# A graph attention and expert kernel: own orders for the second, third and last step, and an end split into graphs and half rows

## The chip, the cores and the metric

The kernel runs on one core of a Trainium2 chip. The metric is device time in microseconds (us) from the start to the end of one execution, lower is better. The core has five engines that run side by side, each with a queue of its own in program order: TensorE (PE, matrix products; its weight loads are shown as PEld), VectorE (DVE), ScalarE (ACT), GpSimd (POOL) and SyncE (SP, which issues most transfers).

## The reference, cut to what matters

There are 128 graphs of 128 nodes with 1024 features. Each goes through a graph attention layer and then through a layer of low-rank experts:

```python
x = x + gnn(layernorm(x), adj, W, a)     # 16 heads of 64: softmax over neighbours, att @ Wh, elu
xn = layernorm(x)
gates = softmax of the 2 largest of (xn[:, 0, :] @ router_w.T), of 8 experts
x = x + xn + sum over chosen experts of gate * up(down(xn))      # rank 16
```

The attention score of a neighbour does not depend on the neighbour's own features here, only on the row, so a row's weights reduce to two numbers per head (an exponential for entries and one for absent entries) and the neighbour sum is a product of the 0/1 adjacency with Wh. The routing of a graph takes only its first row.

## The kernel before, in words

**Steps.** A step q (0 to 63) takes two graphs, 2q and 2q+1, through the product with W (1024 x 1024, float32). It is done by seven block products M1 to M7 instead of eight (sums of blocks of x are made by GpSimd, L462; sums of blocks of W lie in SBUF). From step 2 on, two steps share the products M3 and M5, which are split once more by the same scheme: the joint products I and J (L609), whose weight sums `w_in` are made once by GpSimd (`inner_blocks`, L122 to L125, for the blocks T1 and B22). A block product is 16 matmuls at L530 (a and b halves of 8).

**Behind the product.** ScalarE makes the high part of each of four blocks (`hi0` to `hi3`, L683), VectorE the remainder (`lo0` to `lo3`, L687). One step later come, for the two graphs: weights (`aw`, `pe`, `aw2`: L705 to L733), attention product (`A0`, `A1`: L742), scaling by the weights (`h`, L748, in place in PSUM), elu and residual (`x` L755, `e` L758 on ScalarE, `y` L765, `n` on GpSimd), the variance (`q`, L774 on ScalarE), a copy and a DMA transpose (`t`, L815 and L817) and the copy into `y_t` (`rj`, L821), and the second normalization with the residual (`jn`, L842).

**Experts.** Four graphs make a group g. Its routing runs on VectorE (`choose`, L937 to L944), the rows of the chosen experts are fetched by GpSimd's indirect DMA, then follow the down product (`D`, L1004), the gates (`dn`, L1015), the up product (`U0`, `U1` for the two halves of the columns, L1024) and the addition (`v00` to `v11`, L1033) with the store. The last group uses dense weights instead: `load_all` and `load_router` bring all rows in, `order_all` (L1055) reorders the down rows, `down_dense` (L1064), `gates_dense` and `up_dense` (L1089, L1090) do the rest.

**Order.** All five engines are scheduled by hand: the order in which tasks are issued in the program is the order in each engine's queue. Steps 2 to 63 follow two lists, `EVEN` and `ODD`, in which a name ending in `-` belongs to the step before. Steps 0, 1 and 64 to 65 are ordered by `at_the_ends`, which fills eight gaps between the block products. There `weights`, `update` (scaling to mean of one graph) and the rest run graph by graph whole rows at a time, the tables of the experts are centred in one function (`experts`), and both `inner_blocks` stand in step 1.

**PSUM.** Two pairs of banks (`pw0`, `pw1`) belong to the block products; two more pairs (`ps_d`) serve everything else in turn: the attention product of one graph takes a pair, an up product of four graphs both.

```python
if HALVES["left"] is None:
    two = double(name)
    HALVES["left"] = two[:, 1]
    return two[:, 0]
left, HALVES["left"] = HALVES["left"], None
return left
```

Of the kernel before, what the change touches and what calls it, by code (L numbers as in the profile page):

```python
# [18 lines left out]
NO_ENTRY = -3.0e38  # L19
# [3 lines left out]

EVEN = """
# [11 lines left out]
fe5- M2a h0 rj1- jn1- M2b h1 M6a x0 x1 e0 fe2- y0 ps2- fe8- sc0 n0 M6b hi0 e1  # L36
""".split()
# [3 lines left out]
def adj_ffn_kernel(  # L41
# [117 lines left out]
    def load_counts(g):  # L159
        adj_i = work.tile([P, G, N], I32, tag="adj_i", name="adj_i", bufs=1)  # L160
        nc.sync.dma_start(adj_i, adj[g])
        GRP[g] = {"adj_i": adj_i}

    def load_adj(g):
        adj_f = work.tile([P, G, N], F32R, tag="adj_f", name="adj_f")
        nc.gpsimd.dma_start(adj_f, adj_t[g])
        GRP[g]["adj_f"] = adj_f
# [199 lines left out]
    def experts(part, sums):  # L367

        nonlocal down_row, up_row
# [3 lines left out]
        nc.tensor.matmul(pr[:, ER:ER + E], mean_of, sums, start=True, stop=True)  # L373
        nc.vector.scalar_tensor_tensor(
# [5 lines left out]
        nc.sync.dma_start(router_table, router_k.rearrange("p e k -> p (e k)"))  # L380
        down = down_sb.rearrange("p e r k -> p (e r) k")
# [3 lines left out]
                          down_sb.rearrange("p e r k -> p e (r k)"))  # L385
        rows = work.tile([P, P], I32, tag="hp", name="rows")
# [258 lines left out]
    def project(q):  # L645
# [9 lines left out]
        if q:  # L655
            for names in (("M1", "p1"), ("M6", "u2"), ("M2", "hi0", "sc0"), ("M5", "u4"),
                          ("M7", "c22"), ("M3", "c12"), ("M4", "c21")):
                do(names[0] + "a", names[0] + "b", *names[1:])
                yield
            return  # L660
# [30 lines left out]
    def attention_weights(q):  # L691


        g, first = divmod(2 * q, G)
        st = GRP[g]
        shape = [P, 2, H]
        pair = slice(first, first + 2)
        neg = st["neg"][:, pair, None].to_broadcast(shape)
        rstd = RSTD[q]
        e = small.tile(shape, F32, tag="e", name="e", bufs=2)  # L700
        blocks = e.rearrange("p t (h j c) -> p (t h) j c", h=NH, j=2)
        sc = SC.pop(q)
        for dst, raw in (((blocks[:, 1:], WH[q][:, :, :, SCORES]), (blocks[:, 0], sc)) if q
                         else ((e, sc),)):
            nc.vector.scalar_tensor_tensor(dst, raw, ALPHA, raw, op0=ALU.mult, op1=ALU.max)  # L705
# [3 lines left out]
        p = small.tile([P, 2, 2, H], F32, tag="p", name="p", bufs=2)  # L709
        nc.vector.tensor_tensor(p[:, 0], e, m, ALU.subtract)  # L710
        nc.vector.tensor_tensor(p[:, 1], neg, m, ALU.subtract)
        ATT[q] = p

    def exp_weights(q):

        nc.scalar.activation(ATT[q], ATT[q], AF.Exp)

    def divide_weights(q):

        g, first = divmod(2 * q, G)  # L720
        st = GRP[g]
        shape = [P, 2, H]
        pair = slice(first, first + 2)
        p = ATT[q]
        z = small.tile([P, 2, 2, H], F32, tag="z", name="z", bufs=2)
        nc.vector.tensor_mul(z, p, st["n"][:, :, pair, None].to_broadcast(z.shape))
        den = small.tile(shape, F32, tag="den", name="den", bufs=2)


        nc.vector.scalar_tensor_tensor(den, z[:, 0], TINY, z[:, 1], op0=ALU.add, op1=ALU.add)  # L730
        nc.vector.reciprocal(den, den)
        ATT[q] = small.tile(shape, F32, tag="att", name="att")
        nc.vector.tensor_mul(ATT[q], p[:, 0], den)  # L733
# [11 lines left out]
    def weigh_sum(i):  # L745

        ph = PH[i].rearrange("p j (h f) -> p (j h) f", f=F)
        nc.vector.tensor_tensor(ph, ph, ATT[i // 2][:, i % 2, :, None].to_broadcast([P, H, F]),  # L748
# [75 lines left out]
    def turn_at_end(i):  # L824

        two = double("pt")
        TT[i] = [two[:, h].rearrange("p (c n) -> p c n", c=CPH) for h in range(NH)]
        for h, pt in enumerate(TT[i]):
            for c in range(CPH):
                k = h * CPH + c  # L830
                nc.tensor.transpose(pt[:, c, :], X[i][:, k * P:(k + 1) * P], ident)

    def keep_turned(i):
        y = y_of(i)
        for h, pt in enumerate(TT.pop(i)):
            (nc.vector.tensor_copy if h and i == B - 1 else nc.scalar.copy)(
                y[:, h * CPH:(h + 1) * CPH], pt)

# [42 lines left out]
    def turned_parts(g, last):  # L881

        st = GRP[g]
        n = 1 if last else G - 1
        if not last:
            st["add"] = small.tile([P, G * E + G], F32, tag="add", name="add", bufs=1)
        add = st["add"][:, 0:G * E].rearrange("p (g e) -> p g e", g=G)[:, G - 1:G] if last else (
            st["add"][:, 0:(G - 1) * E].rearrange("p (g e) -> p g e", e=E))
        shape = [P, n, E, KC]
        prod = work.tile(shape, F32, tag="hp", name="prod")  # L890
        router = router_all.rearrange("p (o e k) -> p o e k", o=1, e=E)
        if last:
            pieces = [(pt.rearrange("p (o c) n -> p o n c", o=1)[:, :, 0:1],
                       slice(h * CPH, (h + 1) * CPH)) for h, pt in enumerate(TT[g * G + G - 1])]
        else:
            pieces = [(st["y_t"].rearrange("p k (g n) -> p g n k", g=G)[:, 0:n, 0:1],
                       slice(0, KC))]
        for rows, k in pieces:
            part = prod[:, :, :, k]
            nc.vector.tensor_tensor(part, rows.to_broadcast(part.shape),  # L900
                                    router[:, :, :, k].to_broadcast(part.shape), ALU.mult)
        nc.vector.tensor_reduce(add, prod, AX.X, ALU.add)

    def logits(g):
# [4 lines left out]
        if g < NG - 1:  # L909
            nc.tensor.matmul(st["pl"][:, 0:G * E + G], ones, st["add"], start=True, stop=True)  # L910
            return
        nc.tensor.matmul(st["pl"][:, 0:G * E], ones, st["add"][:, 0:G * E], start=True, stop=True)
        down_dense(g, 2, 2, range(0, 5))
        st["dev"] = single("dev")[:, 0:G]
        nc.tensor.matmul(st["dev"], ones, st["add"][:, G * E:], start=True, stop=True)
        down_dense(g, 2, 2, range(5, KC))
# [44 lines left out]
    def weigh(g):  # L961
# [5 lines left out]
        if g < NG - 1:  # L967
            st["gate"] = own(gate, "gate")
# [88 lines left out]
    def down_dense(g, t, n, chunks=range(8)):  # L1057

        st = GRP[g]
        if "pd" not in st:  # L1060
            st["pd"] = slot_of(0)[:, 0]
        cols = slice(t * P, (t + n) * P)
        for k in chunks:
            nc.tensor.matmul(st["pd"][:, cols], down_all[:, k].rearrange("p e r -> p (e r)"),  # L1064
                             st["y_t"][:, k, cols], start=(k == 0), stop=(k == KC - 1))

    def gates_dense(g):

        st = GRP[g]
        val = st["val"].rearrange("p v g s -> p v (g s)")  # L1070
        hit = small.tile([P, G * TOP], F32, tag="own", name="hit", bufs=2)
        nc.vector.tensor_scalar(hit, val[:, 0], own_order, None, op0=ALU.is_equal)
        nc.vector.tensor_tensor(hit, hit, val[:, 1], ALU.mult)
        gate = small.tile([P, G], F32, tag="gate_all", name="gate_all", bufs=1)
        nc.vector.tensor_reduce(gate, hit.rearrange("p (g s) -> p g s", g=G), AX.X, ALU.add)
        st["dn"] = work.tile([P, G, P], F32, tag="s1", name="dn_all", bufs=2)
        pd = st["pd"].rearrange("p (t n) -> p t n", t=G)
        for t in (slice(0, 1), slice(1, G)):
            nc.vector.tensor_tensor(st["dn"][:, t], pd[:, t],
                                    gate[:, t, None].to_broadcast(pd[:, t].shape), ALU.mult)  # L1080

    def up_dense(g):
        st = GRP[g]
        for t in range(G):
            y = X.pop(g * G + t)
            for h in range(NH):
                cols = slice(h * HALF, (h + 1) * HALF)
                pu = single("pu")
                nc.tensor.matmul(pu, st["dn"][:, t], up_all[:, cols], start=True, stop=True)  # L1089
                nc.vector.scalar_tensor_tensor(y[:, cols], pu, st["rstd"][:, t:t + 1], y[:, cols],  # L1090
                                               op0=ALU.mult, op1=ALU.add)
                (nc.sync, nc.scalar)[h].dma_start(out[g * G + t, :, cols], y[:, cols])
# [90 lines left out]
    def do(q, name):  # L1183

        if name.endswith("-"):
            q, name = q - 1, name[:-1]
# [4 lines left out]
    def between(q):  # L1191

        DOES[q] = tasks(q)
        for name in (EVEN, ODD)[q % 2]:
            if q > 2 or not name.endswith("-"):
                do(q, name)
        if q == NQ - 1:
            load_all()
            load_router()
            order_all()  # L1200

    def at_the_ends(q):

        gaps = [[] for _ in range(8)]
        if q == 0:
            prepare(gaps)
        g, part = divmod(q - 2, 2)
        ffn = 0 <= g < NG
        if ffn and not part:
            gaps[6] += [(logits, g), (choose, g)]  # L1210
        if q < NQ:
# [125 lines left out]
```

## Time and profile before

| what | value |
|---|---|
| median of 3 runs | 1875.3 us (1873.36 to 1875.72) |
| the profiled execution | 1874.31 us, of which the span from first to last instruction is 1872.5 us |
| mean granted TensorE clock | 0.997 |
| busy: PE, PEld, DVE, ACT, POOL | 98%, 80%, 85%, 66%, 62% of the span |
| chain that ended last, by engine | PE 90%; POOL, DVE 3% each; ACT 2% |
| costliest line of the chain | L530, 56% of the span |
| DMA engines | busy 0.5 to 0.65 of the time in most of the span |

The profile is one execution. A row of a group or a queue gives the start, the duration and the count of one kind of instruction, with the line of the kernel that issued it; "[1.48 <-ACT ph L774]" behind it says that the engine was idle for 1.48 us before it and what ended the wait. Matmuls are pipelined, so that the mean duration of one (386 ns at L530) is longer than the distance from one to the next. In the tables of stretches, a busy time equal to the length means that the engine had no gap.

### The profile page before, as it was taken

How to read it: one execution, taken by the hardware profiler on the slowest of the kernel's cores; microseconds unless marked ns; L12 is line 12 of the kernel's file. 1: busy time of each engine (PE TensorE's matmuls, PEld its weight loads, DVE VectorE, ACT ScalarE, POOL GpSimd, SP SyncE). 2: the span in 40 equal slices, each digit the busy share in tenths (PEclk: the TensorE clock that was granted, in tenths of full speed). 3: DMA queues.
4: the chain of work that ended last, by engine and by line, in shares of the span. 5: the costliest groups of instructions: out<-in, count | busy, mean ns of one | idle time of the engine just before them, and what ended most of it. 6: DMA issues, size and time to landing. Idle time of an engine off the chain costs nothing.

```text
span 1872.5 us, 29571 instructions
## 1 busy us (share of the span) xinstructions
PE 1841.8 (98%) x10182; PEld 1504.8 (80%) x10182; DVE 1586.4 (85%) x3386; ACT 1237.5 (66%) x1409; POOL 1159.4 (62%) x1675
## 2 busy tenths in 40 slices
PE   9899999999999999999999999999999999999996
PEld 6788888888888888888888888888888888888883
DVE  6788888888888888888888888888888888888876
ACT  3567666766666666667666667666667766667663
POOL 3567566667566666566666566676666676566660
PEclk9999999999999999999999999999999999999999
DMA  8445656555666655656655666655656555655542
GB/s 318 127 142 172 193 183 202 177 143 176 192 184 194 178 139 183 195 180 187 179 143 186 198 175 189 179 147 186 197 177 181 173 160 183 198 178 180 161 124 101
DMA packets 349100, 330.42 MB, mean 176 GB/s; under 512 B 279196, under 2 KB 281372, under 8 KB 348440
## 3 DMA queue, kind: packets, MB, share of 16 engines
q1 hardware_dynamic: 331224, 286.57, 50.2%
q0 software_dynamic: 17008, 40.91, 7.3%
q8 instruction: 81, 1.33, 0.3%
q10 hardware_dynamic: 720, 1.06, 0.2%
q14 instruction: 67, 0.55, 0.1%
HBM read 194.24 MB, written 68.17 MB: 140 GB/s over the span
## 4 chain that ended last, share of the span: by engine, by line
PE 90%; POOL 3%; DVE 3%; ACT 2%; issue 1%; DMA 1%; SPq 0%; DVEq 0%; ACTq 0%; POOLq 0%
PE pw L530 56%; PE pw L609 17%; PE ph L742 6%; PE pd L1004 3%; PE pu L1024 3%; PE ix L609 3%; POOL down L989 2%; DMA w_sb<-in_w 1%; ACT ph L774 1%; ACT y_t L821 0%; PE pu L1089 0%; POOL xt L462 0%; DVE xn L755 0%; ACT ph L758 0%; DVE ph L748 0%
## 5 line engine op out<-in xcount | busy, mean ns | idle before, releaser
L530 PE MATMUL pw<-w_sb,xt 128*128 128x260 f32 (+1 forms) x4080 | 960.9, 386 | 3.7 <-ACT wh L542 2.7
L530 PEld LDWEIGHTS pw<-w_sb,xt 128*128 128x128 f32 x4080 | 763.9, 190 | 172.9 <-issue 30.0
L989 POOL DMA_INDIRECT down<-table,at_down x248 | 249.3, 1005 | 198.5 <-DVE of_slot L952 117.1
L683 ACT ACTIVATE parts<-wh,rstd 128x512 fp32r<-128x512 f32 x192 | 135.3, 721 | 348.2 <-DVE wh L537 312.3
L821 ACT COPY y_t<-tt 128x2048 uint16<-128x2048 uint16 x126 | 314.5, 2497 | 0.2 <-DMA tt<-halves 0.2
L530 PE MATMUL pw<-w_sb,s 128*128 128x260 f32 (+1 forms) x1088 | 249.7, 382 | 0.0
L815 ACT COPY halves<-xn 128x2048 uint16<-128x2048 uint16 x126 | 237.8, 1888 | 1.3 <-DVE xn L765 1.3
L530 PEld LDWEIGHTS pw<-w_sb,s 128*128 128x128 f32 x1088 | 206.4, 190 | 34.5 <-DVE wh L537 0.9
L462 POOL TENSOR_TENSOR s<-xt 128x512 f32<-128x512 f32 x64 | 83.2, 1300 | 233.4 <-DMA xt<-in_x_t 233.4
L758 ACT ACTIVATE ph<-ph 128x1024 f32<-128x1024 f32 x128 | 130.0, 1015 | 92.8 <-DVE xn L755 85.7
L1033 DVE SCALAR_TENSOR_TENSOR xn<-pu,rstd,xn 128x512 f32<-128x512 f32 x248 | 171.6, 745 | 11.5 <-PE pu L1024 11.4
L765 DVE SCALAR_TENSOR_TENSOR xn<-ph,xn 128x1024 f32<-128x1024 f32 x128 | 155.9, 1218 | 4.6 <-ACT ph L758 4.5
L401 DVE BATCH_NORM_STATS2 stats<-xn 128x6 f32<-128x512 f32 x248 | 158.5, 681 | 0.0
L842 ACT ACTIVATE xn<-xn,off,mul 128x1024 f32<-128x1024 f32 x128 | 157.7, 1234 | 0.0
L748 DVE TENSOR_TENSOR ph<-ph,att 128x1024 f32<-128x1024 f32 x128 | 151.5, 1228 | 6.5
L755 DVE SCALAR_TENSOR_TENSOR xn<-ph,xn 128x1024 f32<-128x1024 f32 x128 | 150.4, 1216 | 0.1
L774 ACT ACTIVATE ph<-xn,acc 128x1024 f32<-128x1024 f32 x128 | 143.4, 1120 | 10.1 <-POOL acc L770 9.7
L687 DVE SCALAR_TENSOR_TENSOR parts<-wh,rstd,parts 128x512 fp32r<-128x512 f32 x192 | 141.1, 749 | 6.5 <-ACT parts L683 2.8
L742 PE MATMUL ph<-parts,adj_f 128*128 128x512 f32 x512 | 143.9, 422 | 2.4 <-DVE xn L1033 2.4
L609 PE MATMUL pw<-w_sb,i 128*128 128x260 f32 x496 | 129.2, 383 | 0.0
L609 PE MATMUL pw<-w_in,s 128*128 128x260 f32 x496 | 129.1, 383 | 0.0
L742 PEld LDWEIGHTS ph<-parts,adj_f 128*128 128x128 f32 x512 | 93.9, 188 | 28.3 <-issue 7.9
(209 smaller groups left out, 2644.1 us busy)
## 6 DMA issues: line engine op xcount, KB each, us to landing
xn<-in_x SPq DMA_DIRECT2D x128, 512.0 KB
xt<-in_x_t SPq DMA_DIRECT2D x127, 512.0 KB
out_y<-xn SPq DMA_DIRECT2D x124, 512.0 KB
adj_f<-in_adj_t POOLq DMA_DIRECT2D x32, 256.0 KB
adj_i<-in_adj SPq DMA_DIRECT2D x32, 256.0 KB
down<-table,at_down POOLq DMA_INDIRECT x248
w_sb<-in_w SPq DMA_DIRECT2D x3, 1040.0 KB
wt_sb<-in_w_t SPq DMA_DIRECT2D x1, 2048.0 KB
```

Of the source, the lines that this page charges most:

```text
L401: nc.vector.bn_stats(st[:, h, :], X[i][:, h * HALF:(h + 1) * HALF])
L530: nc.tensor.matmul(banks[name][:, j, cols], lhs()[:, k, :], w_sb[:, rhs, k, j, cols], start=(fresh and k == 0), stop=(k == KH - 1), skip_g ...
L609: nc.tensor.matmul(bank(name), sums(lhs)[:, k], w_of[rhs][:, k], start=(fresh and k == 0), stop=(k == KI - 1), skip_group_check=not fresh)
L742: nc.tensor.matmul(PH[i][:, h], GRP[g]["adj_f"][:, t, :], PARTS[q][:, s, NH * (i % 2) + h], start=(s == 0), stop=(s == 1))
L748: nc.vector.tensor_tensor(ph, ph, ATT[i // 2][:, i % 2, :, None].to_broadcast([P, H, F]), ALU.mult)
L765: nc.vector.scalar_tensor_tensor(X[i], whole(i), 1.0, X[i], op0=ALU.min, op1=ALU.add, accum_out=acc[:, 0:1])
L774: nc.scalar.activation(whole(i), X[i], AF.Square, bias=acc[:, 1:2], accum_out=acc[:, 2:3])
L815: nc.scalar.copy(halves, X[i].bitcast(U16).rearrange("p (d s) -> p s d", s=2))
L821: nc.scalar.copy(y_of(i).bitcast(U16).rearrange("p k (n s) -> p s k n", s=2), TT.pop(i).rearrange("p (s k) n -> p s k n", s=2))
L842: nc.scalar.activation(X[i], X[i], AF.Identity, bias=GRP[g]["off"][:, t:t + 1], scale=GRP[g]["mul"][:, t:t + 1])
L989: nc.gpsimd.indirect_dma_start(out=st["down"][:, j * R:(j + 1) * R].rearrange("p r k -> p (r k)"), out_offset=None, in_=table, in_offset=b ...
L1033: nc.vector.scalar_tensor_tensor(y[:, cols], st["pu", h][t], st["rstd"][:, t:t + 1], y[:, cols], op0=ALU.mult, op1=ALU.add)
```

## The change

The steps 1, 2 and 63 with 64 get lists of their own. `FIRST` orders steps 1 and 2 together, `LAST` step 63 with everything behind it; a name ending in `+` belongs to the step after. `at_the_ends` keeps only step 0. `experts` is cut into `expert_sums` (`ex`), `center_router` (`er`), `center_down` (`ed`) and `table_rows` (`ei`); `iT` and `iB` are the two `inner_blocks`, `tb` the table sums, `la` a load of adjacencies.

At the end (`at_the_end`) the last two graphs (r = 0, 1) are worked on in half rows (h = 0, 1), and their attention weights one graph at a time (`aw0`, `aw1`). A task `A01` is the attention product of r = 0, half 1; `w`, `E`, `a`, `b` are scaling (from PSUM into SBUF), exponential, and the two parts of elu and residual; `n`, `q`, `s` mean, squares and statistics; `T`, `k` a transpose on TensorE and its copy. The last group is routed as two sets: A (its first two graphs, 124 and 125) and C (the last two). `P`, `R`, `L`, `ch`, `V`, `sp`, `rt`, `wg` are the products with the router, their sum, the logits, the choice, the deviation, the spread, and the gates; `dA`, `d0C`, `d1C`, `g`, `u` are down product, gates and up product of a half row. Of the upper products, `m` scales on ScalarE and `v` adds on GpSimd for set A and for the second column half of the group before (`m0B` to `m3B`, `v0B` to `v3B`, in place of `v10` and `v11`); set C is still added by VectorE. `LW`, `LR`, `OA` are the loads of the dense weights, the router, and `order_all`. The filler products (`stay_busy`) of the old end are gone.

```diff
+FIRST = """
+lt aw M1b A0 pe M1a lz2 rt lx M6a aw2 A1 sq M6b p1 M2b M2a h1 hi0 h0 sc0 x1 e1 u2 ps0 x0 ps1
+lo0 M5b y1 M5a M7a iT e0 u4 n1 ei q1 M7b c22 M3a t1 st0 M3b y0 st1 c12 M4b hi3 t0 iB n0 ps3
+ro0 ps2 M4a ac c21 hi1 M1b+ hi2 aw+ pe+ lt+ q0 tb rj0 ss jn0 lo1 ps0+ rs M1a+ A0+ ex lo2
+aw2+ lo3 p1+ Jt0+ ro1 h0+ ed jn1 an M6a+ er lx+ x0+ M6b+ A1+ rj1 h1+ x1+ e0+ ps1+ u2+ la+
+y0+ M2b+ Jt1+ M2a+ J6+ ro0+ lc e1+ sc0+
+""".split()
...
+LAST = """
...
+fe2- I5- fe1- I2- fe7- Is- I3- lo2- A1 Ie- fe6- Id- hi1- fe3- aw M1b lo1- M1a jn0- pe LW+
+aw2 fe8- p1 A0 h1 M2a x1 M2b h0 rj1- x0 e1 eo y1 hi0 sc0 e0 lo0 y0 M6b M6a wg n1 q1 D t0 u2
+u4 f n0 hi1 dn aw0+ lo1 M7a M7b LR+ q0 pe0+ c22 U0 M4b ss t1 hi3 M4a dw0+ v00 rj0 v01 rdA+
+U1 m1B+ lo3 v1B+ m0B+ c21 aw1+ rj1 A00+ pe1+ hi2 A01+ w00+ w01+ v0B+ A11+ a01+ dw1+ a00+
+E01+ jn1 b01+ m2B+ PA+ w11+ lo2 RA+ E00+ T01+ A10+ m3B+ b00+ w10+ n0+ LA+ OA+ a11+ a10+ q0+
+s0+ E11+ VA+ T00+ dA+ E10+ chA+ k00+ b10+ spA+ b11+ k01+ T10+ T11+ n1+ v3B+ rtA+ wgA+ P11+
+k11+ P10+ gA+ u00A+ q1+ P0+ m00A+ RC+ v2B+ LC+ u01A+ jn0 s1+ rdC+ chC+ VC+ m01A+ v00A+ v01A+
+k10+ d1C+ spC+ rtC+ ac u10A+ d0C+ m10A+ wgC+ gC+ u11A+ j1+ u00C+ m11A+ u10C+ j0+ v10A+ u01C+
+v10C+ v00C+ u11C+ v11C+ v01C+ v11A+
 """.split()
...
+        def attend_half(r, h):
+            if i + r not in PH:
+                PH[i + r] = double("ph")
+            for s in range(2):
+                nc.tensor.matmul(PH[i + r][:, h], GRP[g]["adj_f"][:, 2 + r, :],
+                                 PARTS[p][:, s, NH * r + h], start=(s == 0), stop=(s == 1))
...
+        def above_half(r, h):
+            x = X[i + r][:, at(h)]
+            nc.vector.scalar_tensor_tensor(x, sums[r][:, at(h)], 0.0, x, op0=ALU.max,
+                                           op1=ALU.add)
...
+        def scaled(name, pu, m, of):
+            got["part", name] = work.tile([P, HALF], F32, tag="s1", name="part_up", bufs=2)
+            nc.scalar.mul(got["part", name], pu, of["rstd"][:, m:m + 1])
+
+        def scale_up(s, t, h):
+            scaled((s, t, h), got.pop(("pu", s, t, h)), sets[s][0] + t, st)
+
+        def scale_before(t):
+            scaled(t, GRP[g - 1]["pu", 1][t], t, GRP[g - 1])
+
+        def add_scaled(name, n, h):
+            y = X[n]
+            nc.gpsimd.tensor_tensor(y[:, at(h)], got.pop(("part", name)), y[:, at(h)], ALU.add)
...
     def between(q):
 
         DOES[q] = tasks(q)
-        for name in (EVEN, ODD)[q % 2]:
-            if q > 2 or not name.endswith("-"):
-                do(q, name)
+        if q == 1:
+            DOES[1].update(of_tables())
+            DOES[2] = tasks(2)
         if q == NQ - 1:
-            load_all()
-            load_router()
-            order_all()
...
+            DOES[NQ] = at_the_end()
+        for name in FIRST if q == 1 else LAST if q == NQ - 1 else (EVEN, ODD)[q % 2]:
+            do(q, name)
...
+    for q in range(1, NQ):
+        if q != 2:
             between(q)
```

## The prediction, made before the changed kernel ran

> **What bounds the kernel now.** I read the share of the span first, then TensorE's waits, then stretches of a few microseconds at both ends, then the queues of all engines there. All times are microseconds of the profiled execution.
>
> ```profile
> PE   9899999999999999999999999999999999999996
> ...
> PEclk9999999999999999999999999999999999999999
> ```
>
> TensorE is full in all forty slices but the second and the last. The loop's products (steps 2 to 62) leave nothing that a reordering of other engines could give: the chain of waits passes the attention products of two like steps at 116.79 and 173.04, so 28.1 a step, nearly all of it matmul. Only the ends can pay. TensorE's waits say where they lie:
>
> ```profile
> PE pt L831 <- ACT ph L774: 5.8, 1, 5.8
> PE pd L1004 <- ACT ph L774: 3.3, 5, 1.5
> PE pw L609 <- DVE wh L537: 2.9, 1, 2.9
> PE pw L530 <- ACT wh L542: 2.7, 1, 2.7
> ```
>
> The last two lie at 82.5 and 90.5, in step 2; the first in the tail; 1.5 of the second at 1817.7. The stretches around them (length, then busy time of PE, PEld, DVE, ACT, POOL, granted clock, DMA):
>
> ```profile
> 80.00:85.00 5.00, 2.45 (x12) 1.78 (x10) 4.54 (x10) 0.60 (x2) 4.42 (x5) 0.99 1.02 351
> 85.00:90.00 5.00, 4.81 (x15) 3.99 (x16) 4.79 (x6) 0.14 (x1) 4.74 (x6) 0.67 0.45 145
> 90.00:95.00 5.00, 2.07 (x10) 1.50 (x9) 4.95 (x7) 2.91 (x5) 0.51 (x2) 1.00 0.00 0
> ...
> 1828.00:1840.00 12.00, 7.38 (x33) 4.43 (x32) 9.28 (x21) 7.10 (x6) 0.00 (x0) 1.00 0.45 176
> 1840.00:1848.00 8.00, 2.65 (x11) 2.47 (x12) 5.66 (x7) 3.90 (x6) 0.23 (x1) 0.67 0.00 0
> ...
> 1857.00:1872.50 15.50, 7.93 (x16) 2.71 (x16) 7.09 (x12) 1.68 (x2) 0.00 (x0) 1.00 0.36 135
> ```
>
> At 80 to 95 VectorE and GpSimd are full and TensorE starves; then its clock falls to 0.67. From 1828 no engine is full, and GpSimd is empty: a chain of dependences.
>
> **The head (steps 1 and 2).** TensorE's work is unchanged: the same products, table sums and attention products, in another order. From its first product of step 1 (44.46) to the first joint product of step 2 (93.41) it loses 0.45 + 2.74 + 2.93 in waits, and 16 products at 85.19 take 5.28 where such a row takes 3.51: 1.77. Sum 7.9; without these losses the joint product would start at 85.5. The rest of the step is full already.
>
> Why it starves: VectorE gets to the score operations of step 2 (L705) only at 80.5, behind the iota rows (L389), which waited for GpSimd's first four block sums; and there five operations that take 0.19 each elsewhere take about 1.2 beside the second four. Two pairs from the queues of VectorE and GpSimd:
>
> ```profile
> 81.54 1.26 DVE L706 TENSOR_TENSOR e<-e,rstd 128x32 f32<-128x32 f32 x1
> ...
> 1044.65 0.79 DVE L733 TENSOR_TENSOR att<-p,den 128x32 f32<-128x32 f32 x1
> ```
>
> ```profile
> 80.11 1.29 POOL L123 TENSOR_TENSOR w_in<-w_in,w_sb 128x520 f32<-128x520 f32 x1
> ...
> 1044.05 1.34 POOL L462 TENSOR_TENSOR s<-xt 128x512 f32<-128x512 f32 x1 [7.93 <-DMA xt<-in_x_t]
> ```
>
> The second pair ends together: VectorE is held to the end of GpSimd's sum, then needs its own 0.1.
>
> New order, with row durations. The block sums of T1 (5.4) lie at about 55 to 62, those of B22 at 63 to 69.5, before any score operation of step 2. The last sum of each overwrites a block still in use and waits for M5 (61) and M3 (68): GpSimd's queue behind it (mean, iota, pair sums of step 2) waits too, and those are due later. The table rows (at_r) fall to 63 to 64.5, beside M7. c21 ends at 72.6, so the scores run at 72.7 to 74, low 3 ends at 77.1, and ScalarE's p1 of step 2, behind a rejoin (2.4) and a join (1.15), at 79.9: needed by M2 at 81.5. Centring the table (1.2) and router (0.6) now stands before the second graph's attention products, whose PSUM pair it frees: 80.8 against 81. u2, which the joint product waits for, ends at 84.7 against 85.5; low 0 of step 2 at 86.9 against 87.3. The inputs of step 3, issued after M4, should land 6.3 later as now (issue 78.14, use 84.42), at 77.8, and their two sums be through at 83.5. Router and table stores move behind these on SP; nothing reads them before the row fetches near 100. So every margin holds, by 0.2 to 1.6. I take 7.5 of the 7.9; below, 5 (two margins missed by 1.5); above, 8.
>
> **The tail.** Three parts. First, moving the copy that orders the dense rows (L1055):
>
> ```profile
> 1815.91 2.08 ACT L1055 COPY w_sb<-w_sb 128x1024 f32<-128x1024 f32 x1
> ```
>
> It delays L774, and with it the PSUM that the down products (L1004) wait 1.48 for. Now M6 ends at 1817.5 and the chain D 2.2, M7 3.7, U0 1.07, M4 3.7, U1 1.07 ends at 1829.3, against 1830.95. The copy's new place is behind m3B; its cost there is hidden by the attention products that dA needs anyway.
>
> Second, graph by graph instead of in pairs. Walking the queues (matmuls by L742, 0.47 a half; VectorE half rows 0.62 to 0.75 by L537, L687, L765; ScalarE 0.55 to 0.62 by L426, L683; GpSimd half rows 1.3 by L462): U1 holds both PSUM pairs. A00 waits for m1B and m0B (1830.7); w01 ends at 1832.7. A11 needs the other pair, so m2B and m3B, which stand on ScalarE behind rj1 2.4, pe1 0.2, hi2 0.6, E01 0.55, jn1 1.15 and E00 0.55: 1837.4. Queued behind A11 on TensorE are T01, A10 and all later products; VectorE waits for it from 1836.2. This is a new wait of some 5.8 on TensorE. Then w11, lo2, RA and b00 (with hops) reach 1840.9, w10 1841.7, a11 and a10 1843.1, the choice of set A 2.2: 1845.3; b10, spA, b11 1847.0; gates 1.05, P11, P10, gA 0.85: 1848.9.
>
> From here the set-C chain counts: u00A 0.95, m00A 0.62, jn0 1.15, m01A 0.62, k10 0.55, d1C 1.95 (16 passes at the 0.12 of L831), u10A 0.95, d0C 1.95, then five up halves at 0.95 (L1089), and the last two additions 1.7. With hops and short waits that ends at 1863.8. Routing for C (2.2 + 1.05) lies beside d1C and d0C. Before, the last addition ended here, 3.4 before the span did:
>
> ```profile
> 1866.30 2.00 PE pu L1089 x4
> 1868.30 0.02 issue
> 1868.32 0.75 DVE xn L1090
> ```
>
> So 5.2 gained on this walk. The doubled small operations (weights by graph, choice by set) cost some 4 of VectorE's time, in its idle stretches.
>
> Third, the adds on GpSimd: eight of 1.3. Here a rule speaks against the change. By the Trainium skill (SBUF — State Buffer, "Who interferes with whom") a VectorE instruction with two SBUF inputs and a GpSimd instruction that reads SBUF exclude each other for the whole instruction. The rows above agree (1.26 for 0.19). The new half-row operations, products and choices have mostly two SBUF inputs. By the rule the cost could reach 10.4, if VectorE stood through all eight; by place, v1B and v0B end at 1832.8, as a01 is due, v00A and v01A meet routing C, which has 3 of slack, and only v3B holds the gates of A: 1.2. I take 1.2.
>
> The second rule: the skill (TensorE: Matmul & The Clock Gate, "Why this matters for your kernels") halves the clock after a gap above about 3. Here a gap of 5.78 before L831 left 0.67 over 1840 to 1848. The new gap of 5.8 does the same to A11 up to dA; the 2.1 lost now (L831's first eight 1.97 for 0.97, L1064's eight 3.10 for 2.0) recurs, mostly in front of gA: 1.8 alone, but beside the held gates both together cost 1.9, not 3. By the rule, with a gap in each hand-over keeping it low, the 12 of set C and up products would double (1876); the rows show 1.00 again from 1852 with gaps of 0.5 to 1.3 between, so I take the rows. Tail end 1865.7: 3.4 gained. Ends: 0 (held operations on the path at every add) and 7 (neither penalty, and A11 not held by m3B).
>
> **Sum.** 7.5 + 3.4 = 10.9. The span is 1872.5 in an execution of 1874.31; 1863.4 for such an execution, and the median of the runs shown (1875.3) lies 1.0 higher: 1864.4.
>
> **Rivals.** (1) The tail gives nothing: the A11 wait, the port and the clock take it back. For: three penalties on one chain. Against: none reaches 5.2 alone. 1875.3 - 7.5 = 1867.8. Chance 0.14. (2) The tail is better than walked, A11 running before m3B and the clock holding: 1875.3 - 7.9 - 7 = 1860.4. 0.06. (3) The head's waits only move, to the second attention product or the joint product, whose margins are thin; then just the tail: 1875.3 - 3.4 = 1871.9. 0.05. (4) Slower: a wait that recurs. The loop starts at step 3 with less backlog cleared; if VectorE or GpSimd then come w late in each of 61 steps, the price is 61 w, and above (10.9 + 3.75) / 61 = 0.24 a step the kernel is slower by over 0.2%. For: VectorE waits only 0.2 to 0.25 before many of its PSUM reads. Against: per two steps VectorE has over 6 idle and GpSimd 7.93 in one piece, so a backlog of two or three is worked off in the first pair. With 0.3 a step: 1864.4 + 18.3 = 1882.7. 0.03.
>
> **Numbers.** Likeliest 1864.4, chance 0.72. The range takes the bounds of head and tail and reaches over (1) and to (2): 1860.0 to 1870.0. 0.2% (3.75) is about what a measurement of this kernel tells from no change. Faster by more: the likeliest, (1) and (2), 0.92; within: (3), 0.05; slower: 0.03.
>
> **What would show it.** Right: no TensorE wait above 0.5 and a clock near 1.00 at 80 to 95, joint products starting near 85.5 to 86; down products at once after M6; a TensorE gap of about 5 ending with m3B's scaling; gates of set A beside a GpSimd add with one operation near 1.2; the last addition some 11 earlier. Wrong: a wait of p1 or u2 in the head, waits in every step, half-clock products after the first C down product, or a choice of set C spread over 5 or more beside v00A and v01A.

## The result, and the profile after

After takes 1860.36 us (median of 6 runs, 1858.17 to 1863.02) and before 1875.51 (6 runs) beside it: a ratio of 0.9922, 95% interval 0.991 to 0.9935. The forecast of 1864.4 was 4.0 too high; the range (1860.0 to 1870.0) held the median by 0.4. The profiled execution of after took 1858.17, the least of the six, its span 1856.3. All times below are microseconds of profiled executions unless a median is named.

The slices of the page, as before, with TensorE's row and its clock:

```profile
PE   9999999999999999999999999999999999999997
...
PEclk9999999999999999999999999999999999999998
```

The second slice is full now; the last one is 7 for 6. TensorE's waits in after (who waited, for whom: total, times, longest):

```profile
PE pw L1106 <- DVE xn L1079: 1.9, 1, 1.9
PE pd L986 <- ACT ph L802: 1.6, 4, 0.4
PE ph L1054 <- DVE sums_of L1060: 1.5, 1, 1.5
PE ph L1054 <- ACT part_up L1237: 1.4, 1, 1.4
PE pd_all L1210 <- DVE pr L1185: 1.2, 1, 1.2
```

The two waits of step 2 are gone, and so is the 1.5 before the down products. Behind the kernel's first 5 us, single waits of more than 1.0 are left only in the new end; the 1.6 of L986 are four of at most 0.4. The stretches (length, busy time of PE, PEld, DVE, ACT, POOL, granted clock, DMA share and GB/s):

```profile
80.00:85.00 5.00, 5.00 (x24) 4.14 (x23) 4.03 (x5) 4.09 (x3) 3.98 (x7) 1.00 1.00 297
85.00:90.00 5.00, 5.00 (x24) 4.13 (x24) 4.42 (x8) 4.22 (x9) 3.05 (x5) 1.00 0.66 150
90.00:95.00 5.00, 5.00 (x25) 4.33 (x24) 4.59 (x12) 1.49 (x2) 3.17 (x7) 1.00 0.98 299
1820.00:1830.00 10.00, 5.23 (x22) 3.56 (x19) 7.68 (x23) 9.82 (x12) 2.96 (x4) 0.79 0.26 105
1830.00:1836.00 6.00, 6.00 (x28) 5.08 (x26) 4.80 (x23) 3.40 (x8) 2.81 (x8) 0.78 0.00 0
1836.00:1842.00 6.00, 3.30 (x11) 1.46 (x11) 4.49 (x17) 4.98 (x9) 5.00 (x10) 1.00 0.43 175
1842.00:1848.00 6.00, 6.00 (x39) 4.56 (x39) 1.31 (x6) 2.52 (x5) 1.85 (x2) 1.00 0.29 110
```

At 80 to 95 TensorE is busy without a gap at full clock (before: 2.45, 4.81 and 2.07 of 5). The score operation of step 2 that took 1.26 beside GpSimd's block sums now stands behind them, and the joint product follows without a wait (VectorE, then TensorE):

```profile
72.54 0.19 DVE L735 TENSOR_TENSOR e<-e,rstd 128x32 f32<-128x32 f32 x1
...
84.86 1.11 PE L640 MATMUL pw<-w_in,i 128*128 128x260 f32 x4
```

The down products of the last full group, before first, after second:

```profile
1819.18 2.29 PE L1004 MATMUL pd<-y_t,down 128*32 128x128 f32 x64 [1.48 <-ACT ph L774]
```

```profile
1808.62 1.98 PE L986 MATMUL pd<-y_t,down 128*32 128x128 f32 x64
```

In the end GpSimd works now, ScalarE is nearly full at 1820 to 1830, and the clock is at 0.78 to 0.79 for 16 us. The chain of work that ended last, pieces of it in order of time (start, duration, what), shows what sets the end there:

```profile
1830.76 4.46 PE pd_all L1210 x16
1835.22 0.89 PE pw L1106 x8
...
1840.42 0.95 DVE pr L1181
...
1841.76 2.02 PE pd_all L1210 x16
1843.79 0.86 PE pu L1224 x2
1844.65 1.78 PE pd_all L1210 x16
1846.43 4.31 PE pu L1224 x10
```

It runs through the down products of set A, then through the choice of set C on VectorE, and from d1C (1841.76) on through TensorE without a gap, up to the last two additions:

```profile
1850.76 1.41 DVE L1230 SCALAR_TENSOR_TENSOR xn<-pu,rstd,xn 128x512 f32<-128x512 f32 x2 [0.20 <-PE pu L1224]
```

To place the gain, four marks that every kernel below has: P, the first product of step 1 that follows its wait for `w_sb`; J, the first joint product; D, the first down product of the last full group; E, the end of the last addition on VectorE.

| kernel | J − P | J to D | D to E | E to end | span |
|---|---|---|---|---|---|
| before | 48.95 | 1725.77 | 49.89 | 3.4 | 1872.5 |
| after | 40.56 | 1723.76 | 43.55 | 4.1 | 1856.3 |
| gain | 8.4 | 2.0 | 6.3 | −0.7 | 16.2 |

P itself came 0.16 earlier, which closes the sum. These marks, here and below, are those of one execution of each kernel.

### The profile page after: what moved, and what is told of

Same layout as the page of the kernel before. It is cut to its first block, busy times and chain, and to the rows that moved or that the text cites. A ratio compares the mean times of both kernels' runs of the same rounds, so it can differ in the third digit from the quotient of the medians.

```text
span 1856.3 us, 29668 instructions
## 1 busy us (share of the span) xinstructions
PE 1839.1 (99%) x10196; PEld 1504.2 (81%) x10196; DVE 1578.4 (85%) x3411; ACT 1242.8 (67%) x1423; POOL 1172.0 (63%) x1691
## 4 chain that ended last, share of the span: by engine, by line
PE 93%; POOL 3%; DVE 2%; issue 1%; ACT 0%; DMA 0%; DVEq 0%; POOLq 0%
PE pw L561 58%; PE pw L640 17%; PE ph L770 6%; PE pu L1006 4%; PE pd L986 3%; PE ix L640 3%; POOL down L971 2%; PE pd_all L1210 0%; POOL xt L493 0%; PE pu L1224 0%; ACT ph L802 0%; DVE w_sb L1293 0%; DVE w_sb L306 0%; POOL s L493 0%; PE idle L238 0%
## 5 line engine op out<-in xcount | busy, mean ns | idle before, releaser
L793 DVE SCALAR_TENSOR_TENSOR xn<-ph,xn 128x1024 f32<-128x1024 f32 x126 | 153.2, 1216 | 0.2
L783 DVE SCALAR_TENSOR_TENSOR xn<-ph,xn 128x1024 f32<-128x1024 f32 x126 | 147.9, 1213 | 0.1
```

The source lines that it names most:

```text
L783: nc.vector.scalar_tensor_tensor(X[i], whole(i), 0.0, X[i], op0=ALU.max, op1=ALU.add)
L793: nc.vector.scalar_tensor_tensor(X[i], whole(i), 1.0, X[i], op0=ALU.min, op1=ALU.add, accum_out=acc[:, 0:1])
```

## The experiments

The theory after the result: the gain is the head's lost time (8.4) plus the wait before D plus a shorter chain behind D, which were forecast, and the chain is shorter than forecast because A11 did not wait for m3B. The first rival: what A11 gained was of no use, and the chain is short because the penalties (GpSimd's adds, clock) were small. The second: head and tail do not add, one makes room for the other.

All medians, with the ratio to before on the same chip:

| kernel | median | ratio, 95% interval | J − P | J to D | D to E |
|---|---|---|---|---|---|
| head_only | 1865.58 | 0.9958, 0.9941 to 0.9974 | 40.55 | 1725.74 | 49.76 |
| tail_only | 1867.62 | 0.997, 0.9962 to 0.9979 | 46.84 | 1725.80 | 44.13 |
| a11_held | 1861.23 | 0.9935, 0.9918 to 0.9951 | 40.55 | 1724.36 | 45.81 |
| adds_on_vector | 1865.49 | 0.9959, 0.9945 to 0.9973 | 40.55 | 1724.0 | 50.57 |
| adds_on_vector2 | 1868.87 | 0.9965, 0.9953 to 0.9978 | 40.55 | 1723.5 | 54.98 |
| no_clash | 1858.50 | 0.991, 0.9894 to 0.9927 | 40.56 | 1724.5 | 42.83 |
| clock_fill | 1857.52 | 0.9908, 0.9891 to 0.9925 | 40.55 | 1724.0 | 41.99 |
| order_later | 1871.97 | 0.9986, 0.9978 to 0.9994 | 47.48 | 1723.6 | 49.56 |
| after_again | 1859.81 | 0.9923, 0.991 to 0.9937 | 40.56 | 1724.6 | 43.50 |
| both | 1857.45 | 0.9908, 0.9893 to 0.9923 | 40.56 | 1724.0 | 41.98 |
| b_on_vector | 1861.97 | 0.9933, 0.9917 to 0.9948 | 40.56 | 1725.3 | 46.06 |

**Head alone.** The kernel before with `FIRST` and its pieces; the loop and the old end stay.

```diff
-        for name in (EVEN, ODD)[q % 2]:
-            if q > 2 or not name.endswith("-"):
-                do(q, name)
...
+        for name in FIRST if q == 1 else (EVEN, ODD)[q % 2]:
+            do(q, name)
```

> Steps 1 and 2 in the new order, the end as before. Theory (head and tail are separate and add up): the first joint product starts at about 85 as in the changed kernel, the stretch from the first down product D of the last step to the last addition stays at 49.9 us, the time is 8.5 us below before: 1867. Rival (the loop passes on part of the head's gain only through the new end, or eats some of it): above 1869, or a different length of the loop between.

J − P is that of after to 0.01, and D to E is that of before to 0.13. The median is 8.5 below before on the same chip, as the theory had it.

**Tail alone.** After with the old steps 1 and 2 (the old `at_the_ends` is put back for them).

```diff
-        for name in FIRST if q == 1 else LAST if q == NQ - 1 else (EVEN, ODD)[q % 2]:
+        for name in LAST if q == NQ - 1 else (EVEN, ODD)[q % 2]:
...
```

> Steps 0 to 2 in the order of before, the last step and the end as changed. Theory: the first joint product starts at 93.4, from D to the last addition 43.5 us in place of 49.9 and the 1.5 us wait before D is gone: 7 to 8 us below before, 1868. Rival (the end gains only because the head left less backlog): above 1871.

D to E is 44.13, within 0.6 of after. The old head shows its waits again, and the clock falls after them:

```profile
80.00:85.00 5.00, 3.55 (x16) 2.77 (x15) 4.50 (x9) 0.74 (x2) 4.52 (x5) 1.00 1.00 335
85.00:90.00 5.00, 2.80 (x13) 2.09 (x11) 4.86 (x6) 0.33 (x1) 4.82 (x6) 1.00 0.46 167
90.00:95.00 5.00, 3.54 (x10) 2.87 (x11) 4.34 (x7) 3.58 (x6) 1.62 (x5) 0.74 0.00 1
```

VectorE and GpSimd are the full engines in the first two rows, as before. The median is 6.4 below before, less than the 7 to 8 forecast; with the 8.5 of the head alone that makes 14.9, against 15.2 for both. So the halves are independent: neither needs the other, and the second rival falls.

One thing was not expected: from P to J the old head lost 6.3 here, 6.9 in order_later and 8.4 in before, with the same program order, while the new one takes 40.55 or 40.56 in every kernel. Most of the spread is the clock. The 16 products behind the wait for `wh`, in before and then in order_later:

```profile
85.19 5.28 PE L530 MATMUL pw<-w_sb,xt 128*128 128x260 f32 x16 [2.74 <-ACT wh L542]
```

```profile
85.02 3.77 PE L530 MATMUL pw<-w_sb,xt 128*128 128x260 f32 x16 [2.73 <-ACT wh L542]
```

The same wait was followed by slow products in the one execution (clock 0.67 at 85 to 90) and not in the other (1.00), and 5.28 for 3.77 is the difference of 1.5 between the two heads. In tail_only the slow products stand behind J, and J to D is longer there by some 1.6. So about 1.5 of the head's 8.4 hangs on what the clock does in the old head of that execution.

**A11 held until m3B.** After with one small ScalarE operation behind m3B that reads the PSUM which A11 is going to overwrite, so that A11 waits as the prediction walked it.

```diff
-E01+ jn1 b01+ m2B+ PA+ w11+ lo2 RA+ E00+ T01+ A10+ m3B+ b00+ w10+ n0+ LA+ OA+ a11+ a10+ q0+
+E01+ jn1 b01+ m2B+ PA+ w11+ lo2 RA+ E00+ T01+ A10+ m3B+ LT+ b00+ w10+ n0+ LA+ OA+ a11+ a10+ q0+
...
+        def late_read():
+            nc.scalar.copy(small.tile([P, 1], F32, tag="row", name="late", bufs=1),
+                           PH[i][:, 0, 0:1])
```

> As changed, with one more read of one column of the first graph's attention product by ScalarE, behind m3B, so that its PSUM pair is not free when A11 comes and A11 must take the pair that m2B and m3B free, as the prediction had it. Theory (the prediction's step failed because A11 took the first graph's pair, freed by w01): A11 starts with m3B's end, some 4 us later than now, T01 and w11 some 1.7 us later, and the last addition 1.5 to 2.2 us later; 1862. Rival (A11 has slack, the miss lies elsewhere): the last addition within 0.5 us.

The same product in TensorE's queue, after first, a11_held second (start, duration, then in brackets the idle time before it and what ended it):

```profile
1824.17 0.70 PE L1054 MATMUL ph<-parts,adj_f 128*128 128x512 f32 x2 [1.47 <-DVE sums_of L1060]
```

```profile
1829.14 1.22 PE L1054 MATMUL ph<-parts,adj_f 128*128 128x512 f32 x2 [5.22 <-ACT late L1066]
```

The gap forecast was 5.8; held, it is 5.22, and the clock falls to 0.50 at 1830 to 1836. D to E grows by 2.26, the slower clock included, a little above the theory's 1.5 to 2.2, and the rival's 0.5 falls: of the 4.0 that A11 comes later behind D, 1.7 or more lies in slack. In after A11 waits for `sums_of` (w01), the reader of the first graph's PSUM, and not for an upper product: it got the pair that w01 frees. That is the step of the prediction that was wrong.

**The eight adds on VectorE.** After with each of the eight scaled upper products added by one VectorE operation, as set C's are, where m stood.

```diff
...
-            does.update({f"m{t}B": (scale_before, t), f"v{t}B": (add_before, t)})
+            does.update({f"m{t}B": None, f"v{t}B": (add_before, t)})
-                does.update({f"m{t}{h}A": (scale_up, "A", t, h)})
+                does.update({f"m{t}{h}A": None})
```

> As changed, but the eight half-row additions of set A and of the group before are done by VectorE straight from PSUM; ScalarE's eight scalings and GpSimd's eight sums are left out. Theory (the end is a chain with idle time on VectorE, the split is what pays): VectorE has 5.3 us more, of which some 2 to 3 us falls on the chain, less the 0.9 us for which pr stood beside a GpSimd sum; last addition 1 to 2.5 us later, 1862. Rival (VectorE bounds the end, the move to ScalarE and GpSimd is what pays): 5 us later, 1865.

7.0 longer behind D, neither number. The order was badly chosen: v00A, on VectorE, stood ahead of the join of graph 124, which ScalarE does, so the first half row of graph 124 got its expert addition before its normalization (this part of the computation is changed), the join waited for v00A and its store (2.77 on ScalarE), and d1C waited 2.74 for k10 and then took 3.68 where it takes 2.02 in after (clock 0.72 at 1848 to 1854). So it was made again with v00A and v01A behind the join:

> After, but the eight scaled additions of the upper products that ScalarE and GpSimd did are single VectorE operations (0.75 each) again; those of the graph 124's half rows stand behind its join on VectorE's queue. All outputs are the reference's. Main theory (VectorE is close to the bound of the tail, so its queue grows): eight times 0.75 is 6.0 of new VectorE work, less some 1.3 of waits beside GpSimd's sums that go away: the last addition 3 to 5 later than in after, 1863 to 1865. Rival (the tail is bound by the chain of TensorE, ScalarE and small operations, so VectorE has room): 0 to 1.5 later, 1860 to 1862.

Worse still, 11.4 behind D: now u01A waits 2.86 in TensorE's queue for PSUM that VectorE frees only behind the set's choice (v00A ends at 1846.09, L1185 at 1846.15, when u01A starts), and d1C a further 1.91 for k10. Neither run gives a clean price of VectorE's time. In both, A00 waits 2.2 for an addition by VectorE where it waits 1.35 for a scaling by ScalarE in after. That the eight adds are wanted off VectorE less for their 6.0 of busy time than because a scaling on ScalarE frees PSUM sooner, while an addition waits for its turn behind the small operations, is a reading of these waits and not shown.

**The four of the group before alone.** v0B to v3B on VectorE where m0B to m3B stood; set A as in after.

> After, but only the four upper halves of the group before (scaled by ScalarE, added by GpSimd) are single VectorE additions again (0.75 each), each where the scaling stood. Main theory (VectorE's queue feeds the attention sums of graphs 124 and 125 here, and U1's PSUM comes free later by an addition of 0.75 behind VectorE's queue than by a scaling of 0.62 on ScalarE): A01 waits some 2 instead of 1.35 and the granted clock falls as it did with all eight on VectorE; the last addition 2 to 4 later than in after, 1862 to 1864. Rival (what cost 7 to 11 with all eight on VectorE was the set-A half, by the late PSUM of its upper products): 0 to 1 later, 1860.4 to 1861.4.

2.5 behind D (2.56 against after_again, which ran beside it), as the theory had it:

```profile
1823.91 1.52 PE L1054 MATMUL ph<-parts,adj_f 128*128 128x512 f32 x4 [2.16 <-DVE xn L1257]
```

This is A00 and A01, which waited 1.35 in after. The median is 2.2 above after_again. The clock is 0.50 at 1830 to 1836 and the down products of set A take 5.53 instead of 4.67.

**GpSimd's add held back.** In after the last operations of set C's choice lie beside v00A. Rows of VectorE's queue in after, then of GpSimd's:

```profile
1840.33 1.02 DVE L1181 TENSOR_TENSOR pr<-top 128x2 f32<-128x2 f32 x1
1841.46 0.16 DVE L1185 TENSOR_TENSOR pr<-pr,pl 128x2 f32<-128x2 f32 x1
```

```profile
1840.07 2.50 POOL L1247 TENSOR_TENSOR xn<-part_up,xn 128x512 f32<-128x512 f32 x2
```

An operation of two elements takes 1.02, and it ends as the first of GpSimd's two adds does (1840.07 + 1.25 = 1841.32, against 1841.35). The row before it (L1179, one input) is not held.

```diff
-k11+ P10+ gA+ u00A+ q1+ P0+ m00A+ RC+ v2B+ LC+ u01A+ jn0 s1+ rdC+ chC+ VC+ m01A+ v00A+ v01A+
-k10+ d1C+ spC+ rtC+ ac u10A+ d0C+ m10A+ wgC+ gC+ u11A+ j1+ u00C+ m11A+ u10C+ j0+ v10A+ u01C+
+k11+ P10+ gA+ u00A+ q1+ P0+ m00A+ RC+ v2B+ LC+ u01A+ jn0 s1+ rdC+ chC+ VC+ m01A+
+k10+ d1C+ spC+ AS+ v00A+ v01A+ rtC+ ac u10A+ d0C+ m10A+ wgC+ gC+ u11A+ j1+ u00C+ m11A+ u10C+ j0+ v10A+ u01C+
...
+        def after_spread(s):
+            held = small.tile([P, 1], F32, tag="row", name="held", bufs=1)
+            nc.gpsimd.tensor_scalar(held, got["pr", s][:, 0, 0:1], 1.0, None, op0=ALU.mult)
```

> After, with GpSimd's two additions v00A and v01A held (by a tiny GpSimd operation that reads the set-C probabilities) until those probabilities are there. Main theory (a VectorE operation with two SBUF inputs is held while GpSimd adds half rows, and the held operation is on the path to d1C): the operation that took 1.02 takes 0.15, d1C starts 0.5 to 0.9 earlier, 1859.5 to 1859.9. Rival (d1C is bound by ScalarE's k10 just as closely, at about 1841.2): the operation is short but d1C starts 0 to 0.3 earlier, 1860.1 to 1860.4.

```profile
1841.57 0.15 DVE L1181 TENSOR_TENSOR pr<-top 128x2 f32<-128x2 f32 x1
1841.82 0.16 DVE L1185 TENSOR_TENSOR pr<-pr,pl 128x2 f32<-128x2 f32 x1
1842.53 0.17 DVE L1200 RECIPROCAL val<-val 128x2 f32<-128x2 f32 x1 [0.55 <-ACT val L1194]
1842.72 0.79 DVE L1201 TENSOR_TENSOR val<-pr,val 128x2 f32<-128x2 f32 x1
1843.44 1.30 DVE L1204 TENSOR_SCALAR hit<-val,own_order 128x4 f32<-128x4 f32 x1
```

The clash has moved on, to L1201 and L1204 of this kernel (0.79 and 1.30), where it costs nothing: VectorE's next operation behind the gates, `dn_all`, waits 1.80 for the down product anyway. d1C starts 0.75 earlier behind D and now waits 0.72 for k10 on ScalarE (1.22 for `pr` in after); D to E is 0.72 shorter. But 0.2 of the 0.75 lies ahead of the edit: the down products of set A took 4.43 for 4.67 in this execution, and u00A starts 28.0 behind D for 28.2. So the hold is worth some 0.5, about what k10 leaves (in after it ends at 1841.18, and L1185 at 1841.62). That is the low end of the main theory's 0.5 to 0.9, with k10 close behind, as the rival said. The median, 1858.50, is below the numbers of both, and its interval overlaps that of after; it settles nothing here.

**TensorE kept warm.** After with 5, 6 and 7 products of the identity where TensorE stood idle; their result is never read. (The old end had three such products, L215 at 1850 to 1852, which the change left out.)

```diff
-U1 m1B+ lo3 v1B+ m0B+ c21 aw1+ rj1 A00+ pe1+ hi2 A01+ w00+ w01+ v0B+ A11+ a01+ dw1+ a00+
+U1 m1B+ lo3 v1B+ m0B+ c21 aw1+ rj1 F1+ A00+ pe1+ hi2 A01+ F2+ w00+ w01+ v0B+ A11+ F3+ a01+ dw1+ a00+
...
+        def fill(n):
...
+            for _ in range(n):
+                nc.tensor.matmul(turned[0][:, 1, 0:P], ident, ident, start=True, stop=True)
```

> After, with 5, 6 and 7 identity products (their result is never read) where TensorE stood idle after U1, after A01 and after A11. Main theory (the granted clock of 0.78 to 0.79 at 1820 to 1836 comes of those idle stretches, and the slow products are on the path): clock near 1.00 there, the down products of set A 3.9 instead of 4.67, the last addition 0.8 to 1.5 earlier, 1858.9 to 1859.6. Rival (ScalarE and VectorE bound that stretch): the clock rises but the last addition moves by less than 0.3, 1860.1 to 1860.4; if the fillers delay A01, A11 or T01, up to 0.5 later.

```profile
1820.00:1830.00 10.00, 8.99 (x60) 7.11 (x56) 7.76 (x23) 9.68 (x12) 2.96 (x4) 1.00 0.26 105
1830.00:1836.00 6.00, 5.05 (x25) 3.90 (x25) 5.59 (x27) 4.16 (x11) 2.82 (x8) 1.00 0.00 0
```

The clock stays at 1.00 and the down products of set A, 4.67 in after, take 3.72:

```profile
1830.10 3.72 PE L1216 MATMUL pd_all<-y_t,w_sb 128*128 128x256 f32 x16
```

D to E is 1.56 shorter, just above the 0.8 to 1.5 forecast. VectorE's and ScalarE's busy times at 1820 to 1830 are the same to 0.15, and yet the end moved by far more than the rival's 0.3: these engines did not set it there, and the rival falls. The small operation of set C is no longer held either (0.15): the choice has moved ahead of v00A, and d1C waits 0.39 for k10. So 1.56 is what clock and clash together can give until k10 is reached.

**Both, beside after.** No new edit: the two above together, with after run again on the same chip.

> After with both edits: the identity products in the idle stretches and GpSimd's v00A and v01A held until the set-C probabilities are there. Main theory (both edits free the same place, the start of d1C, which ScalarE's k10 then bounds: with the identity products alone that wait for k10 was already 0.39 and the held operation had already moved away): no more than with the identity products alone, 2.5 to 3.2 below after_again, the last addition 41.7 to 42.1 after D. Rival (the two gains of 1.6 and 0.7 add): the last addition 41.2 after D, 3.3 to 3.9 below after_again.

> After itself, unchanged, beside the two below on one chip, since after and the kernels compared with it ran on different chips so far. Both theories: 1860 to 1861; D to the last addition 43.5.

Both: 1857.45 (1857.25 to 1857.53), after beside it 1859.81 (1858.96 to 1861.93). D to E is 41.98, that of the identity products alone (41.99): the main theory, though the median's 2.4 falls just short of its 2.5 to 3.2. Two ways lead to d1C, and the down products of set A lie ahead of both: one through the choice of set C, up to L1185, which is the last to read the logits in the PSUM pair that d1C then takes; one through ScalarE's join and k10, the copy that d1C reads. Holding v00A frees the first alone, and with a warm clock that one is no longer the later. after_again shows it from the other side. In its profile the small operation is free (0.15), but the clock is lower than in after (0.71 and 0.64), the down products of set A take 5.11, and d1C waits 0.66 for k10; D to E is 43.50 against 43.55. One penalty stood in for the other. This kernel and the one with the identity products alone are the fastest here; it is 2.4 below after beside it, and 0.92% below before (0.77 to 1.07).

**The copy moved, alone.** The kernel before with `order_all` behind the attention weights of step 63.

```diff
-            order_all()
...
+                if q == NQ:
+                    gaps[0].append((order_all,))
```

> The kernel before with one edit: the copy that orders the dense rows (2.08 on ScalarE) moved from before the last joint product's softmax to behind the attention weights of step 63. Main theory (the 1.48 wait before the down products is that copy's and nothing waits behind its new place): the down products start 1.5 to 2.0 earlier and the last addition too, 1873.3 to 1873.8. Rival (in the old end's order the copy in its new place holds ScalarE's exponentials, which that end waits for): down products earlier, the last addition 0 to 0.5 earlier, 1874.8 to 1875.3.

D starts without its wait. A new wait of TensorE stands in the copy's new place:

```profile
PE pw L1064 <- ACT w_sb L1055: 3.1, 1, 3.1
...
PE pt L831 <- ACT ph L774: 2.2, 2, 2.0
```

Before, L831 waited 5.8 and L1064 1.8; now it is 2.2 and 3.1. The wait of 3.1 has taken the place of time that would have been waited anyway, and D to E is 49.56 against 49.89. J to D is 2.2 shorter, above the 1.48. But the kernels with the copy moved lie between 1723.5 and 1725.3 (tail_only, with its slow products behind J, is apart) and the two with it in place at 1725.7 and 1725.8: a mean gain of 1.6. The profiled execution moved by 4.1, of which J − P makes 1.5 without an edit there: the old head's own spread. The median moved by 3.3, with an interval of 1.1 to 4.1. So the main theory's place is right, and its 1.5 to 2.0 agree with the marks (1.6 up to D, 0.3 behind it) and lie within the interval; the median alone would say more.

## Why the prediction was right, and where it was not

The range was right by 0.4. Its lower end stands for the best head and the best tail (7, with neither penalty and A11 not held) and for rival (2), which had a chance of 0.06. The likeliest story, with A11 waiting for m3B and the penalties on top, did not happen; that the number fell inside the range is in part luck.

**The head (forecast 7.5, measured 8.4): right, and shown.** All four losses named were there to be had: no wait above 0.5, clock 1.00, J at 84.86 against 85.5 to 86. The term was 0.9 too small: 0.4 that I had taken off the 7.9 for margins, and 0.5 outside the losses that I had summed. Of these, 0.3 is overlap: a row of 16 products shows 3.67, but the next row starts 3.51 after it, so that each of the first two waits cost 0.16 more than its idle time (78.78 to 85.19 is 3.51 and 2.90, for an idle time of 2.74); the rest I did not trace. The margins held. u2 ends at 84.71, as walked, 0.15 ahead of J; the attention product of the second graph starts at 80.23, after the router's centring has ended (79.53). The waits did not move, so rival (3) falls. Two readings were wrong without harm: at 90 to 95 only VectorE is full, GpSimd is busy for 0.51 of 5; and two of the five held operations (L726 and L730, at 84.69 to 87.14) stand beside the block sums of step 3, not beside the second four.

**The wait before D (forecast 1.65 of the tail): right.** Gone in after and, alone, in order_later; J to D is 1.6 shorter on the mean of the kernels with the copy moved.

**A11 waits for m3B: wrong.** The prediction said: "A11 needs the other pair, so m2B and m3B". A11 took the pair of the first graph and waited 1.47 for w01. Restoring the wait costs 2.26 from D to E.

**The rest of the chain behind D.** The walk, penalties included, had 48.2 from D (1817.5) to E (1865.7); measured 43.55, 4.65 less. It splits at u00A, the first upper product of set A. With A11 held, u00A starts 31.0 behind D, where the walk with its penalties had 33.3 (1848.9 + 1.9 − 1817.5): 2.3. Of these, 0.4 lie ahead of A11 (19.5 behind D, walked 19.9); from A11 to u00A the held kernel takes 11.5, which is the walk without its 1.9 of penalties, although the clock was at 0.50 at 1830 to 1836. Without the hold u00A starts at 28.2: another 2.8, of which 0.5 is lost again by E. From u00A to E the walk had 14.9 and the held kernel takes 14.8; that is in part chance, since the terms listed for this stretch add to 15.2 before any hop. So half of the error is A11, and most of the other half penalties that did not come on top: the theory after the result and its first rival each explain half.

**GpSimd's adds (forecast 1.2, at v3B beside the gates of A): the place wrong, the size too large.** The Trainium skill's rule (SBUF — State Buffer, "Who interferes with whom") holds in the rows: the operation with two SBUF inputs goes to 1.02, its neighbour with one does not. v2B and v3B ran at 1834.93 to 1837.43, and the last gate operation of A with two SBUF inputs (L1201) had started just ahead, at 1834.86; one operation of the choice of C was held instead, at a price of some 0.5, and in after_again none that d1C waited for. The product L1128 ahead of that choice was held too (0.84, and 0.26 in b_on_vector, where GpSimd adds nothing then); no run frees it alone. I had given the choice 3 of slack, since its gates are needed late; d1C takes the PSUM pair that the choice reads up to L1185, which I had not counted, so up to there it had none.

**The clock (forecast 1.8 alone): the mechanism right, the cause of the gap wrong.** The gap of 5.8 did not come, and the clock fell all the same, to 0.78 in after, after gaps of 1.35, 1.47 and 1.95. Here the runs differ from the skill's rule (TensorE: Matmul & The Clock Gate, "Why this matters for your kernels") with its gap of about 3; with those gaps filled to 0.4 or less the clock stayed at 1.00. But such gaps need not lower it: in the old end of before, with these, it was at 1.00 from 1830 to 1842.

```profile
1832.52 1.20 PE L742 MATMUL ph<-parts,adj_f 128*128 128x512 f32 x4 [1.50 <-DVE xn L1033]
1834.59 1.17 PE L742 MATMUL ph<-parts,adj_f 128*128 128x512 f32 x4 [0.87 <-DVE xn L1033]
1837.59 1.99 PE L1064 MATMUL pw<-y_t,w_sb 128*128 128x256 f32 x8 [1.83 <-ACT y_t L821]
```

Together with the two old heads, where a wait of 2.7 lowered it once and once not, this says that the length of the gaps alone does not decide. In after the clock cost at most 1.56, with the clash in it. The prediction set no price on leaving out the old end's three products without a reader.

**Rival (2)**, the tail better than walked with A11 before m3B, is what happened, apart from the clock; its 1860.4 is within 0.1 of the median, with 7.9 and 7 where the marks say 8.4 and 7.6. **Rival (4)**, a wait in every step, did not appear: J to D is shorter, not longer.

What stays open: what decides whether the clock falls after a given wait; what the last 0.2 of the head are; and the price of the eight adds by VectorE in an order made for it. That the span ends 4.1 behind E and not 3.4 lies mostly in the stores: in after five of them keep the DMA engines full from 1850.8 to 1854.3, 2.1 behind E, and in before the last two end at 1870.7, 1.6 behind E. No run was made on it.

## What to carry to other kernels

When a walk says that a product waits for a buffer, ask which buffer it will get: here it was the one that came free first, not the other of the two, and this single wait was half of the error. Before a loss is priced or called slack, follow every way to the next instruction on the bounding engine: a second way 0.4 behind (k10 behind the choice of C) caps what freeing the first is worth. In this hand-ordered end, where TensorE was idle in pieces of 1.3 to 2, a few products without a reader paid for themselves (1.5 for 18 products).

## What the runs showed of the hardware

TensorE's clock fell to between 0.64 and 0.79 in after and after_again (1820 to 1836) with no gap above 1.95 in the stretch. A wait of 2.7 in the old head was followed by a clock of 0.67 in before and of 1.00 in order_later. An operation of 128x2 elements on VectorE took 1.02 while GpSimd was adding half rows, and 0.15 where GpSimd's add came later (no_clash) or the operation earlier (clock_fill); a TENSOR_SCALAR with an SBUF operand beside its input was held too (1.30 in no_clash, 0.22 in after).
